# A transformer block in hand-ordered beats: maxima rows sent first, attention rows normalised and transposed earlier

## The chip, the cores and the metric

The kernel runs on one core of one Trainium2 chip. The metric is the device time of one execution in microseconds (us), the median of several runs. The profiles are one execution each.

## The reference

One diffusion-transformer block over a batch of 16 sequences of 256 tokens with 256 channels and 16 heads of 16 channels, all in fp32. Biases, and the first line's `silu`, stand as in the reference:

```python
shift_a, scale_a, gate_a, shift_m, scale_m, gate_m = split(silu(c) @ W_mod + b_mod, 6)
q, k, v = heads(modulate(ln(x), shift_a, scale_a) @ W_qkv + b_qkv)
x = x + gate_a * (softmax(q k^T / 4) v @ W_proj + b_proj)         # self-attention
q = heads(ln(x) @ W_qc + b_qc);  k, v = heads(ln(context) @ W_kvc + b_kvc)
x = x + softmax(q k^T / 4) v @ W_cproj + b_cproj                  # attention to 256 context rows
x = x + gate_m * (gelu(modulate(ln(x), shift_m, scale_m) @ W_mlp1 + b_mlp1) @ W_mlp2 + b_mlp2)
```

## The kernel before

The work is cut into 32 **units**: for every batch row one self-attention (`s`) and one attention to the context (`c`). The order is s0 to s3, then s4, c0, s5, c1 and so on to s15, c11, and then c12 to c15. So from unit 4 on, `s` and `c` alternate up to unit 27 and the rest are `c`. After the units comes the MLP over all batch rows; the set-up before them and a small part of the MLP lie beside the first and last units.

A unit takes eight **beats**; `beat(n, k)` issues everything that belongs to beat k of unit n. Each of TensorE, VectorE (DVE), ScalarE (ACT), GpSimd (POOL) and SyncE (SP) gets its instructions in exactly the order in which the Python code issues them (`InOrder`, lines 39 to 53), and goes through them in that order. So the place of a call in `beat` is its place in the queues of all engines that it uses, and moving a call past another one moves it there too.

Several units are in work at once. In beat k of unit n:

- `visit(n, k)` (lines 1011 to 1026) issues the scores `s` of four heads of unit n+1, for one half of its tokens, and takes their maxima on DVE (`mx`, in `s_tile`); then the transposed scores `st` of two heads of unit n. These contain a row of ones times a row of negative maxima, so that ACT can take the exponential (`pt`) of all of it in one instruction. `st` and `s` have one PSUM buffer each, so scores wait for the maximum of the beat before.
- Beats 0 and 4 hold `av_part`: the products of `pt` and the values (`o`), copied to `oT` by ACT.
- Beats 1 and 5 transpose the maxima (`psm`); `m_send` negates them (`m`) and sends two rows into the queries by DMA from SP. Those sent in beat 1 are read by `st` in beats 4 to 7 of the same unit, those of beat 5 in beats 0 to 3 of the next.
- Beats 6 and 2 transpose the attention result of unit n (first half) and unit n-1 (second half) back to tokens (`psA`); `norm` divides by the sum that came along as a seventeenth column (`rc`, then `A`, on DVE).
- `aT` is the second transposition of unit n-1 (`psT_as`, `psT_ac`), of `A` to channels: `halves()` on TensorE, `evac()` on ACT (`y_as`, `y_ac`), `cut()` on POOL, which splits it into a high and a low part (`xTh`, `xTl`). The projection `ps_P` of beat 7 and of beat 1 of the next unit reads both.
- The layer norm of an `s` or a context input (`ln[0]`), its transposition `T[0]` (`psT_s`, `psT_c`) and the layer norm and transposition of the query rows of a `c` unit (`ln[1]`, `T[1]`: `rs_q`, `xn_q`, `psT_q`) run two to four units ahead. For batch rows 0, 1, 14 and 15 the latter are `late`: `ln[1]` in beat 4, `T[1]` in beat 6 of the same unit (units 2, 4, 27 and 28).
- `Q`, `K`, `V` are the projections for units n+2 and n+3 (`ps_q`, `ps_k`, `ps_v`), in twelve matmuls a half. `high()` and `low()` make their two parts (`h_`, `l_`), `send_high()` and `send_low()` issue four and two DMAs on SP. `load(u)` issues the load of a later unit's input.

Projections and transpositions use 64 of the 128 rows of TensorE each; `lane0` works on one half and `lane1` on the other. `beside(a, b)` interleaves two lists, one for each half, by counted steps: a projection matmul counts 1, a transposition `HALF`.

```python
HALF = 0.53
def beside(a, b):
    ab, at = [chain(*a), chain(*b)], [0, 0]
    while min(at) < 1e9:
        i = at[1] < at[0]
        at[i] += next(ab[i], 1e9)
```

`take(x, 5)` is the next five steps of a list; what is left goes to the next beat (`rest_x`, `rest_y`). The two halves of one transposition write one PSUM bank, and the second half waits for the last instruction of the first (`half_turns`, line 322). PSUM for transpositions, `psm` and `o` comes from two buffers used in turn (`SHORT`), that for projections from two others (`LONG`).

Of the kernel before, what the change touches and what calls it, by code (L numbers as in the profile page):

```python
# [21 lines left out]
def pixart_block(  # L22
# [45 lines left out]
    def ps_gen(name, tag=None):  # L68


        if tag is None and ps_turn[0] is not None:
            ps_turn[0] ^= 1
            tag = (SHORT, LONG)[ps_turn[0]]
        tag = tag or SHORT
        return psum.tile([P, 512], F32, tag=tag, name=name, bufs=2)
# [25 lines left out]
    def tok(ap, b):  # L101
        return ap[b].rearrange("(t p) h -> p t h", p=P)

    def load_x(b):
        X[b] = work.tile([P, NT, H], F32, tag="x", name=f"x_{b}", bufs=5)
        SP.dma_start(X[b], tok(x, b))
# [344 lines left out]
    def take(it, n):  # L451
        for _ in range(n):
            yield next(it, 1)
# [8 lines that stand above are left out]
# [82 lines left out]
    def load(u):  # L544
        if u.kind == "s":
            load_x(u.b)
        else:
            u.ct = work.tile([P, NT, H], F32, tag="c", name=f"c_{u.b}")
            SP.dma_start(u.ct, tok(ctxt, u.b))
# [148 lines left out]
    def m_send(u, hf):  # L698
        m = work.tile([P, P], F32R, tag="m", name=f"m_{u.n}_{hf}", bufs=1)
        at = 96 * hf  # L700
        ACT.mul(m[at:at + 16], u.pm[at:at + 16, :P], -1.0)
        for par in range(2):
            SP.dma_start(u.q[par * 64 + 63:par * 64 + 64, 4 * hf:4 * hf + 4, :].bitcast(F32),
                         m[at + par * 8:at + (par + 1) * 8].bitcast(F32))

    def t_part(u, pair, par, st):


        for c in range(NT):
            PE.matmul(st[:, par, c * N:(c + 1) * N],  # L710
                      u.k[par * 64:par * 64 + 64, pair, c * P:(c + 1) * P],
                      u.q[par * 64:par * 64 + 64, pair, :], start=True, stop=True)
            if c == 0:
                yield
        yield

    def exp(u, pair, st):
        u.pt[pair] = work.tile([P, 2, NT, N], F32, tag="pt", name=f"pt_{u.n}_{pair}", bufs=5)
        ACT.activation(u.pt[pair].rearrange("p r c n -> p (r c n)"), st.rearrange("p r n -> p (r n)"),
                       AF.Exp, scale=SCALE)  # L720
# [9 lines left out]
    def in_turn(*pieces):  # L730

        for _ in range(2):
            for f in pieces:
                next(f)
# [273 lines left out]
    def unit(n):  # L1008
        return units[n] if 0 <= n < nu else None

    def visit(n, k, home=sp):


        v, e = unit(n + 1), k
        s = []
        if v:
            s = [s_tile(v, e // 2, par, e % 2, par, home) for par in range(2)]
        if n < 0:
            in_turn(*s)
            return  # L1020
        bank = sp if n == nu - 1 and k % 2 else st
        t = [t_part(units[n], k, par, bank) for par in range(2)]
        in_turn(*s)
        in_turn(*t)
        later.append(lambda: exp(units[n], k, bank))

    none = (), ()
    rest_x = rest_y = iter(())

    def beat(n, k):  # L1030
        nonlocal rest_x, rest_y
        if n < 0:
            visit(n, k, (st, sp)[k % 2])
            return
        cur, prev, nxt = unit(n), unit(n - 1), unit(n + 1)
        q2, q3, q4 = (v if v and v.n >= m else None
                      for v, m in zip(map(unit, (n + 2, n + 3, n + 4)), (1, 2, 3)))
        p1, p2, p3 = (v and v.post for v in map(unit, (n - 1, n - 2, n - 3)))
        apart = n > nu - 4
        if n - 2 > nu - 5:  # L1040
            p2 = None
        if n - 3 > nu - 5 or p3 and p3.hurry:
            p3 = None
        lc = q4 if q4 and q4.kind == "c" else None
        ls = q4 if q4 and q4.kind == "s" else None
        lx = q3 if q3 and q3.kind == "c" else None
        late = lx and lx.b in (0, 1, B - 2, B - 1)
        early = lc if lc and lc.b not in (0, 1, B - 2, B - 1) else None
        if k == 0 and q2:
            q2.K.high()  # L1050
            q2.K.send_high()
        if k == 2 and p2:
            p2.end()
        if k == 4 and q2:
            q2.Q.high()
            q2.Q.send_high()
        home = sp
        if nxt and n * 8 + k >= nu * 8 - 17 and k % 2:
            home = ps_gen("s0", LONG), ps_gen("s1", LONG)
        visit(n, k, home)  # L1060
        exps()
        if k == 0:
            if prev:
                av_part(prev, 2)
                av_part(prev, 3)
            if q2:
                q2.K.low()
                q2.K.send_low()
            if p3:
                p3.add()  # L1070
            if ls and n > 0:
                load(ls)
            if lc:
                lc.ln[0].steps[0]()
            if p1:
                p1.gate()
        elif k == 1:
            m = m_halves(cur, 1) if cur else none
            x, y = lane0(q2 and q2.Q), lane1(p2)
            beside([m[0], x], [take(y, 4), m[1], y])  # L1080
            if cur:
                m_send(cur, 1)
            if lc:
                lc.ln[0].steps[1]()
                lc.ln[0].steps[2]()
        elif k == 2:
            T = q3.T[0].halves() if q3 else none
            A = p1.halves(1) if prev else none
            x, y = lane0(q2 and q2.V), lane1(q2 and q2.Q)
            beside([T[0], take(x, 5), A[0]], [A[1], take(y, 5), T[1]])  # L1090
            rest_x, rest_y = x, y
            if q3:
                q3.T[0].evac()
                q3.T[0].cut()
            if p2 and p2.hurry:
                p2.add()
        elif k == 3:
            if prev:
                p1.norm(1)
            beside([rest_x], [rest_y])  # L1100
        elif k == 4:
            if cur:
                av_part(cur, 0)
                av_part(cur, 1)
            if q2:
                q2.Q.low()
                q2.Q.send_low()
            if p3:
                p3.store()
            if late:  # L1110
                for f in lx.ln[1].steps:
                    f()
            if ls and not late:
                ls.ln[0].steps[0]()
                ls.ln[0].steps[1](False)
        elif k == 5:
            m = m_halves(nxt, 0) if nxt else none
            aT = p1.aT.halves() if prev else none
            x, y = lane0(q3 and q3.K), lane1(q2 and q2.V)
            beside([m[0], take(x, 4), aT[0], take(x, 3)], [aT[1], take(y, 1), m[1], take(y, 6)])  # L1120
            rest_x, rest_y = x, y
            if prev:
                p1.aT.evac()
                p1.aT.cut()
            if nxt:
                m_send(nxt, 0)
            if ls and late:
                for f in ls.ln[0].steps:
                    f()
            elif ls:  # L1130
                ls.ln[0].pow()
                ls.ln[0].steps[2]()
            if early:
                early.ln[1].steps[0]()
            v = unit(n + 5)
            if v and v.kind == "c":
                load(v)
        elif k == 6:
            if cur:
                cur.post.begin()  # L1140
            T = lx.T[1].halves() if lx else none
            A = cur.post.halves(0) if cur else none
            beside([A[0], take(rest_x, 5), T[0]], [T[1], take(rest_y, 5), A[1]])
            if q2:
                q2.V.keep()
            if early:
                early.ln[1].steps[1]()
                early.ln[1].steps[2]()
            if prev and apart:
                p1.proj(0)  # L1150
                p1.proj(1)
        elif k == 7:
            beside([lane0(None if apart else p1)], [lane1(q3 and q3.K)])
            if lx:
                lx.T[1].evac()
                lx.T[1].cut()
            if prev and apart:
                p1.end()
                p1.add()
                p1.store()  # L1160
            if cur:
                cur.post.norm(0)
# [97 lines left out]
```

## Time and profile before

| | |
|---|---|
| median of 3 runs | 805.89 us (802.38 to 806.07) |
| profiled execution | 800.28 us, span 798.2 us |
| mean granted TensorE clock | 0.995 |
| busy share of the span | TensorE 96%, DVE 74%, ACT 70%, POOL 66% |
| unit 0 begins / MLP alone begins | about 37 us / about 602 us |

A busy share is a mean over parts with different limits; a step of the loop is judged by which engine ends last in its beat. The page's rows give the granted clock in tenths for 40 slices of the span. In a row of a timeline stand the start and the duration in us, engine, line, operation, `out<-in` tiles, shapes and the count of merged instructions; in brackets the engine's idle time before it and what ended that. In a row of windows stand the stretch, its length, the busy time of each engine with its count of instructions, the granted clock, the DMA share and GB/s. In a row of waits stand who waited for whom, the total in us, the times and the longest. All operations are recorded under one line (51, in `InOrder`), so rows are told apart by their tiles.

### The profile page before, as it was taken

The page shows a single profiled execution, that of the slowest core. Times are in us where ns is not written, and L with a number is a line of the kernel's source. Part 1 is how long each engine was busy: PE and PEld are TensorE (multiplying, and loading weights), DVE is VectorE, ACT ScalarE, POOL GpSimd, SP SyncE. Part 2 cuts the span into 40 slices and gives each one's busy share as a digit, 9 for nine tenths or more (in the row PEclk, how much of TensorE's full clock was granted, in tenths as well). Part 3 has the DMA queues.
Part 4 walks back from the last instruction along what each step waited for, and adds up shares of the span by engine and source line. Part 5 has one row for each costly group of instructions (what it writes and reads, how often), then busy time and mean ns, then how long its engine had stood idle before and what let it go on. Part 6 is the DMA issues. An engine that isn't in the chain of part 4 may idle for free.

```text
span 798.2 us, 24978 instructions
## 1 busy us (share of the span) xinstructions
PE 766.0 (96%) x10066; PEld 656.9 (82%) x10066; DVE 589.3 (74%) x1027; ACT 562.0 (70%) x961; POOL 528.4 (66%) x497
## 2 busy tenths in 40 slices
PE   8999899999999999999999999989889999999997
PEld 8778777887877887877888878767669999999997
DVE  5877678888888888888888898776664656656662
ACT  4268587887877877888788888767556666666663
POOL 6756858595766858567595877864546656666653
PEclk9999899999999999999999999999999999999999
DMA  6554344434354544535435554534211321312211
GB/s 208 143 159 123 107 110 121 121 109 144 104 143 108 146 127 109 158 96 146 123 109 150 144 151 136 148 100 115 74 43 42 93 61 60 80 60 61 81 42 52
DMA packets 89942, 87.96 MB, mean 110 GB/s; under 512 B 9506, under 2 KB 85572, under 8 KB 89828
## 3 DMA queue, kind: packets, MB, share of 16 engines
q1 hardware_dynamic: 89364, 85.58, 38.2%
q8 instruction: 80, 1.31, 0.7%
q0 software_dynamic: 192, 0.52, 0.2%
q14 instruction: 34, 0.28, 0.1%
q10 hardware_dynamic: 272, 0.26, 0.1%
HBM read 26.97 MB, written 8.46 MB: 44 GB/s over the span
## 4 chain that ended last, share of the span: by engine, by line
PE 63%; DVE 15%; POOL 9%; issue 5%; ACT 5%; DMA 2%; SPq 1%; POOLq 0%; ACTq 0%; DVEq 0%
PE o L51 14%; PE s L51 12%; PE st L51 7%; DVE mx L51 7%; DVE xn_m L51 4%; PE ps_P_s L51 3%; PE ps_P_c L51 3%; PE ps_v_c L51 3%; POOL hl L51 3%; PE ph L51 3%; PE ps_v_s L51 2%; POOL x L51 2%; PE ps_kc L51 2%; PE ps_q L51 2%; PE ps_qc L51 2%
## 5 line engine op out<-in xcount | busy, mean ns | idle before, releaser
L51 DVE TENSOR_REDUCE mx<-s 128x4 f32<-128x1024 f32 (+1 forms) x257 | 308.3, 1201 | 98.0 <-PE s L51 94.7
L51 ACT ACTIVATE pt<-st 128x1024 f32<-128x1024 f32 x252 | 258.5, 1026 | 49.2 <-PE st L51 37.8
L51 PE MATMUL s<-big 63*128 63x256 f32 (+1 forms) x1024 | 123.8, 314 | 12.0 <-DVE mx L51 10.9
L51 POOL TENSOR_TENSOR hl<-hf,hh 128x512 fp32r<-128x512 f32 x64 | 89.0, 1402 | 54.4 <-ACT hh L51 54.2
L51 PE MATMUL o<-pt,v 128*32 128x256 f32 x2048 | 123.8, 382 | 0.4 <-DVE A_c L51 0.4
L51 PEld LDWEIGHTS s<-big 63*128 63x128 f32 (+1 forms) x1024 | 81.1, 187 | 50.0 <-DVE mx L51 22.3
L51 PE MATMUL st<-big 64*128 64x256 f32 (+1 forms) x1024 | 110.1, 284 | 4.7 <-ACT pt L51 3.1
L51 PEld LDWEIGHTS o<-pt,v 128*32 128x32 f32 x2048 | 60.4, 109 | 41.7 <-PE st L51 0.7
L51 PEld LDWEIGHTS st<-big 64*128 64x128 f32 (+1 forms) x1024 | 83.4, 187 | 8.2 <-ACT pt L51 3.7
L51 ACT ACTIVATE hf<-ph,bT 128x256 f32<-128x256 f32 x120 | 50.3, 473 | 27.6 <-PE ph L51 27.4
L51 ACT COPY oT<-o 128x512 f32<-128x512 f32 x63 | 36.9, 586 | 45.9 <-PE o L51 45.9
L51 ACT ACTIVATE hh<-ph,bT 128x256 fp32r<-128x256 f32 x120 | 50.4, 472 | 22.8 <-PE s L51 8.3
L51 PE MATMUL ph<-wqch,wself 128*128 128x256 f32 x256 | 51.5, 284 | 0.0
L51 PE MATMUL ph<-wkch,wself 128*128 128x256 f32 x256 | 51.4, 285 | 0.0
L51 PE MATMUL s<-big,hh 128*128 128x256 f32 x256 | 46.7, 281 | 0.0
L51 PE MATMUL st<-big,hh 128*128 128x256 f32 x256 | 46.5, 281 | 0.0
L51 DVE TENSOR_SCALAR xn_m<-x,mv_m,rs_m 128x256 f32<-128x256 f32 x32 | 38.4, 1239 | 10.8 <-POOL rs_m L51 10.8
L51 POOL CAST xTh_ac<-y_ac 128x512 fp32r<-128x512 f32 x15 | 9.2, 614 | 54.5 <-ACT y_ac L51 54.5
L51 PE MATMUL ps_k<-xTh_s,wself 64*128 64x256 f32 (+1 forms) x232 | 42.8, 298 | 0.0
L51 POOL CAST xTh_c<-y_c 128x512 fp32r<-128x512 f32 x16 | 9.8, 610 | 48.8 <-ACT y_c L51 48.8
L51 PEld LDWEIGHTS ph<-wqch,wself 128*128 128x128 f32 x256 | 41.6, 189 | 0.4 <-issue 0.4
L51 PEld LDWEIGHTS ph<-wkch,wself 128*128 128x128 f32 x256 | 41.5, 189 | 0.3
(226 smaller groups left out, 2553.0 us busy)
## 6 DMA issues: line engine op xcount, KB each, us to landing
big<-h_kc SPq DMA_DIRECT2D x64, 128.0 KB
big<-h_qc SPq DMA_DIRECT2D x64, 128.0 KB
big<-h_k SPq DMA_DIRECT2D x62, 128.0 KB
big<-h_q SPq DMA_DIRECT2D x62, 128.0 KB
big<-l_k SPq DMA_DIRECT2D x32, 128.0 KB
big<-l_q SPq DMA_DIRECT2D x32, 128.0 KB
c<-in_ctx_dram SPq DMA_DIRECT2D x16, 256.0 KB
g<-gd SPq DMA_DIRECT2D x16, 256.0 KB
```

Source lines behind the costliest of these rows:

```text
L51: i = f(*a, **k)
```

## The change

Four things move; no instruction is added or removed, and the sizes stay.

1. In beat 1, `m_send(cur, 1)` stands ahead of `q2.K.send_low()` and `load(ls)`, which move from beat 0 to after it.
2. `p1.norm(1)` moves from after `visit(n, 3)` to before it: on DVE, `rc` and `A` of the second half stand ahead of the maximum of beat 3.
3. `p1.aT`, its transpositions, its copy and its cut, moves from beat 5 to beat 3.
4. The halves of transpositions in beats 2, 3, 5 and 6 stand at other places of their lists; beat 5 takes eight steps of the projections and leaves four to beat 6, where it took seven and left five.

```diff
@@ beat(n, k), ahead of the visit
+        if k == 3 and prev:
+            p1.norm(1)
         visit(n, k, home)
         exps()
@@ k == 0
             if q2:
                 q2.K.low()
-                q2.K.send_low()
             if p3:
                 p3.add()
-            if ls and n > 0:
-                load(ls)
@@ k == 1
             if cur:
                 m_send(cur, 1)
+            if q2:
+                q2.K.send_low()
+            if ls and n > 0:
+                load(ls)
@@ k == 2
-            beside([T[0], take(x, 5), A[0]], [A[1], take(y, 5), T[1]])
+            beside([T[0], take(x, 1), A[0], take(x, 4)], [take(y, 4), T[1], take(y, 1), A[1]])
@@ k == 3
+            aT = p1.aT.halves() if prev else none
+            beside([take(rest_x, 7), aT[0]], [take(rest_y, 3), aT[1], take(rest_y, 4)])
             if prev:
-                p1.norm(1)
-            beside([rest_x], [rest_y])
+                p1.aT.evac()
+                p1.aT.cut()
@@ k == 5
-            aT = p1.aT.halves() if prev else none
-            beside([m[0], take(x, 4), aT[0], take(x, 3)], [aT[1], take(y, 1), m[1], take(y, 6)])
+            beside([m[0], take(x, 8)], [take(y, 5), m[1], take(y, 3)])
-            if prev:
-                p1.aT.evac()
-                p1.aT.cut()
@@ k == 6
-            beside([A[0], take(rest_x, 5), T[0]], [T[1], take(rest_y, 5), A[1]])
+            beside([T[0], A[0], take(rest_x, 4)], [take(rest_y, 4), T[1], A[1]])
```

## The prediction

> **What bounds the kernel now.** I read the page first, then the waits, then the timeline of one unit, engine by engine. The page gives the shares and the granted clock; the waits name the pair of engines that holds the loop.
>
> ```profile
> PE 766.0 (96%) x10066; PEld 656.9 (82%) x10066; DVE 589.3 (74%) x1027; ACT 562.0 (70%) x961; POOL 528.4 (66%) x497
> PEclk9999899999999999999999999999999999999999
> PEld s L51 <- DVE mx L51: 22.3, 52, 1.7
> ```
>
> TensorE is busy for 96% of the span, so only stretches where it waits, or is held by another engine, can be shortened. The wait that holds it inside the loop is the scores (s) on the maximum (mx). The next rows are unit 13, whose keys and values come from the context; beats 2 to 6 begin just ahead of each mx.
>
> ```profile
> 270.00 1.22 DVE L51 TENSOR_REDUCE mx<-s 128x4 f32<-128x1024 f32 x1
> 271.84 1.23 DVE L51 TENSOR_REDUCE mx<-s 128x4 f32<-128x1024 f32 x1 [0.62 <-PE s L51]
> 272.98 0.25 DVE L51 RECIPROCAL rc_s<-psA_s 128x16 f32<-128x16 f32 x1
> 273.26 0.42 DVE L51 TENSOR_TENSOR A_s<-psA_s,rc_s 128x256 f32<-128x256 f32 x1
> 273.66 1.23 DVE L51 TENSOR_REDUCE mx<-s 128x4 f32<-128x1024 f32 x1
> 276.26 1.22 DVE L51 TENSOR_REDUCE mx<-s 128x4 f32<-128x1024 f32 x1 [0.59 <-PE s L51]
> 278.28 1.23 DVE L51 TENSOR_REDUCE mx<-s 128x4 f32<-128x1024 f32 x1
> ...
> 271.27 0.22 PE L51 MATMUL psA_s<-ident,oT 64*128 64x64 f32 x1
> 271.31 0.49 PE L51 MATMUL s<-big 63*128 63x256 f32 x4
> 273.12 0.50 PE L51 MATMUL s<-big 63*128 63x256 f32 x4 [0.25 <-DVE mx L51]
> ```
>
> From mx to mx the beats take 1.84, 1.82, 2.60 and 2.02 us. Scores of 0.49, a start 0.04 later (271.31 + 0.49 = 271.80, mx at 271.84) and a maximum of 1.23 make a cycle that TensorE cannot undercut: about 1.82. Beats 2 and 3 lie on this floor; in beat 3 TensorE even idles 0.25. Beat 4 is TensorE's own (32 matmuls of o), and beat 5 is 0.20 above the floor. So a step has a price in beat 3 if it delays mx, and a gain in beat 5 if it lightens TensorE.
>
> **Part 1: the second normalisation ahead of the maximum of beat 3.** Now rc and A follow mx of beat 3 and cost nothing: beat 4 is TensorE's. Moved ahead, they wait for the last transposition of psA in beat 2, and behind them wait mx and so the scores of beat 4. From rc to the next mx is 273.66 - 272.98 = 0.68, while DVE's idle time there is 0.62 and partly over before psA is done. The psA transpositions end at 271.27 + 0.22 = 271.49. The re-placed halves of beat 2 change that:
>
> ```profile
> 269.76 0.59 ACT L51 COPY t_c<-ps_P_c 128x512 f32<-128x512 f32 x1 [0.16 <-PE ps_P_c L51]
> 270.40 0.38 PE L51 MATMUL ps_v_c<-wvch,xTh_c 64*128 64x256 f32 x1
> 271.87 0.27 PE L51 MATMUL ps_v_c<-wvcl,xTh_c 64*128 64x256 f32 x1
> ...
> 272.58 0.28 PE L51 MATMUL ps_v_c<-wvch,xTl_c 64*128 64x256 f32 x1
> ```
>
> The first V matmul waits for t_c (269.76 + 0.59 = 270.35). Before, both lists of beat 2 stood still then; after, three Q matmuls are issued ahead of that point. The pace is (272.58 - 271.87) / 6 = 0.12 a matmul, and the code counts a transposition at 0.53 of one, 0.06. From 270.40 on, the second list still holds two matmuls and eight transpositions, 0.74; the last starts at 271.08 and ends at 271.30. I take 271.37, between that and 271.49, because the halves now run beside matmuls and not beside each other. Then mx of beat 3 starts at 271.37 + 0.04 + 0.68 = 272.09, or 0.25 later than now. Bounds: 0.06 if psA is done when mx of beat 2 ends (271.22 + 0.68), 0.37 at 271.49. TensorE's beat 3, with seven matmuls and four transpositions a half (9.1 x 0.12 = 1.1 after 0.5 of scores and exponent matmuls), stays under the new 2.07. It reaches the transposes of A after three matmuls, at 271.87 + 0.36 = 272.23, when A is ready (272.08), so the V and Q matmuls queued behind them do not wait. The cost is paid in 25 units (1, 3, 5 to 26, 29): 25 x 0.25 = **+6.2 us** (1.5 to 9.2).
>
> **Part 2: the attention rows leave beat 5.**
>
> ```profile
> 275.85 0.59 ACT L51 COPY oT<-o 128x512 f32<-128x512 f32 x1 [0.80 <-PE o L51]
> 276.49 0.27 PE L51 MATMUL psT_as<-ident,A_s 64*128 64x64 f32 x1
> 277.72 0.27 PE L51 MATMUL ps_v_c<-wvch,xTh_c 64*128 64x256 f32 x1
> 273.12:281.56 8.44, 8.36 (x129) 6.86 (x130) 7.64 (x14) 6.81 (x11) 7.16 (x8) 1.00 0.36 96
> sum 110.39, PE 109.32 PEld 89.69 DVE 97.12 ACT 88.76 POOL 91.67; mean PE 8.41 PEld 6.90 DVE 7.47 ACT 6.83 POOL 7.05
> ```
>
> psT_as needs the PSUM buffer that the copy oT frees at 276.44, so TensorE starts it late and ends its list at 277.72 + 0.27. In beat 3 it takes the buffer of the transposes psT_s instead, copied by then. Without it beat 5 falls to the floor: 2.02 to 1.82. Another 0.04 goes in beat 4, because y_s, now transposed sooner, lets the exponential of beat 3 end sooner. So beats 4 to 7 of such a unit take 8.20 and not 8.44. The sum row is the 13 odd units 1 to 25: 110.39 - 13 x 8.20 = **-3.8 us**. On ScalarE the copy of the attention rows (0.59) now stands ahead of Q's high part and the exponential of beat 4; the idle 0.80 ahead of oT covers it. If that cover were gone, beat 5 would take 0.59 more.
>
> The other units, which prepare a self-attention unit, are the windows of beats 4 to 7 of units 14 and 10, with the sum of the 11 even units 6 to 26:
>
> ```profile
> 289.92:298.56 8.64, 8.64 (x136) 7.09 (x138) 7.33 (x15) 6.82 (x12) 4.35 (x5) 1.00 0.48 134
> 221.44:230.79 9.35, 8.98 (x136) 7.30 (x138) 7.56 (x15) 7.05 (x12) 4.33 (x5) 1.00 0.47 131
> sum 97.41, PE 96.88 PEld 79.48 DVE 81.31 ACT 76.88 POOL 47.73; mean PE 8.81 PEld 7.23 DVE 7.39 ACT 6.99 POOL 4.34
> 217.81 1.20 SPq L51 DMA_DIRECT2D big<-l_k  x2
> 219.73 1.42 SPq L51 DMA_DIRECT2D big<-m  x2
> 222.31 0.35 PE L51 MATMUL st<-big 64*128 64x256 f32 x1 [0.37 <-ACT h_q L51]
> ```
>
> **Part 3: maxima rows first on SP.** In unit 10 the m rows are issued at 219.73, after key parts and the load, and beat 4's st, which reads them, starts only at 222.31, half a microsecond late. (The releaser named had long ended; I read it as m's landing.) Sent ahead of the two low key parts and the load, they go at about 217.81, 1.9 sooner, and the stall ends. What is late next is DVE's mx of beat 5, behind the statistics of x: unit 14, which has no stall, still takes 8.64. So nine units come to 8.64 and the two without statistics (24, 26) to 8.20: 9 x 8.64 + 2 x 8.20 = 94.2, **-3.2 us**. The key parts moved back are read a unit later, and x, loaded about one beat later, is read in beat 4: nothing is paid there, as long as x lands within three microseconds.
>
> **Part 4: POOL.** The cut of the attention rows moves ahead of rs_q and xn_q in the four units (2, 4, 27, 28) that normalise the query rows in beat 4; there TensorE already waits for xn_q.
>
> ```profile
> 84.24 0.71 POOL L51 TENSOR_TENSOR rs_q<-rs_q,mhalf 128x2 f32<-128x2 f32 x1 [1.28 <-DVE rs_q L51]
> 513.88 0.71 POOL L51 TENSOR_TENSOR rs_q<-rs_q,mhalf 128x2 f32<-128x2 f32 x1 [0.73 <-DVE rs_q L51]
> 517.07 0.61 POOL L51 CAST xTh_as<-y_as 128x512 fp32r<-128x512 f32 x1
> 517.77 1.30 POOL L51 TENSOR_TENSOR xTl_as<-y_as,xTh_as 128x512 fp32r<-128x512 f32 x1
> 535.06 0.71 POOL L51 TENSOR_TENSOR rs_q<-rs_q,mhalf 128x2 f32<-128x2 f32 x1
> ```
>
> The cut takes 2.0 (517.07 to 519.07); the idle time ahead of rs_q takes in 1.28 of it in unit 2, 0.73 in unit 27 and none in unit 28; unit 4, where it is longer than the cut, loses nothing. Delay 0.7 + 0 + 1.3 + 2.0 = 4.0, less about 0.5 for lighter beats 6: **+3.5 us** (0 to 4).
>
> **Part 5: the last two units.**
>
> ```profile
> 574.12 0.46 PE L51 MATMUL psT_ac<-ident,A_c 64*128 64x64 f32 x4
> 575.83 0.94 PE L51 MATMUL ps_warm<-wz 128*128 128x128 f32 x6 [0.73 <-ACT y_ac L51]
> 589.22 0.39 PE L51 MATMUL ph<-wkch,wself 128*128 128x256 f32 x1
> 589.98 0.42 DVE L51 TENSOR_TENSOR A_c<-psA_c,rc_c 128x256 f32<-128x256 f32 x1
> ```
>
> In unit 30 the transposes leave a beat in which ps_warm waits 0.73 for their copy, about -1.0. In unit 31 they move ahead of ph, which could start at 589.22, and wait for A_c (590.40): +1.2. Together **+0.2**.
>
> **Sum.** 6.2 - 3.8 - 3.2 + 3.5 + 0.2 = +2.9 us on the profiled execution's 800.28 (its span 798.2 and 2.1 around it): 803.2. The runs shown have a median of 805.89, 0.7% above that execution, so I forecast 805.89 + 2.9 = 808.8. About 4 us, 0.5%, is what a measurement of this kernel can tell from no change: the forecast is no change.
>
> **The rivals.** *Slower: the halves run badly beside matmuls.* In beat 5 the mixed list took 276.49 to 277.99, 1.50, for 9.1 counted steps, 0.16 a step and not 0.12. If beat 2 goes at that rate, the 6.2 steps after 270.40 take 1.0, psA ends near 271.6, and mx of beat 3 is 0.5 late: 25 x 0.25 more, 815. It decides wherever psA ends after 271.49. Against it: the wait for oT's buffer explains part of the slow list.
>
> *The clock.* After the stalls of unit 2 the granted clock fell; after equal stalls of unit 28 it did not:
>
> ```profile
> 86.00:90.00 4.00, 2.94 (x33) 2.63 (x32) 1.46 (x4) 1.61 (x2) 3.92 (x5) 0.55 0.40 132
> 90.00:94.00 4.00, 4.00 (x47) 3.78 (x48) 2.26 (x4) 2.22 (x4) 3.81 (x5) 0.60 0.02 4
> 533.00:537.00 4.00, 2.48 (x37) 1.98 (x33) 3.08 (x9) 1.91 (x5) 3.79 (x4) 1.00 0.59 160
> ```
>
> Part 4 lengthens unit 28's stall by 2.0. A fall as in unit 2 loses up to 0.45 x 4 + 0.40 x 4 = 3.4; part of that lies in the stall itself, and I take 2: 810.8. [...]
>
> *Faster: the normalisation fits DVE's gap.* If psA is done by 271.22, Part 1 costs 1.5 and not 6.2; if POOL, relieved of its wait for y_ac, also has the cut out of the way in the late units, Part 4 goes to 0: 808.8 - 4.7 - 3.5 = 800.6. For it: the 0.62 of idle DVE. Against: t_c holds V until 270.40.
>
> *The m rows change nothing,* since st waits for something else: Part 3 is lost, 812.
>
> **How the numbers follow.** Forecast 0.42 (of it 0.33 same, 0.06 slower, 0.03 faster); bad mixing 0.18, slower; clock 0.10 (0.06 slower, 0.04 same); fits the gap 0.20 (0.14 faster, 0.06 same); m rows 0.10 (0.07 slower, 0.03 same). Faster 0.17, same 0.46, slower 0.37. The range runs from the faster case, 800, to a little past bad mixing, 816. The forecast's own range, from its bounds, is 804 to 812.
>
> **What would show it.** Right: in ordinary units rc and A stand between the maxima of beats 2 and 3, beat 3 takes about 2.07 and beat 5 of odd units 1.82; st in beat 4 never starts more than 0.4 after its scores; rs_q of units 27 and 28 waits behind xTl_as and xTl_ac. Wrong: beat 3 still at 1.84, or beat 2 grown above 1.9; beat 5 still at 2.0; unit 10 still above 9 us in beats 4 to 7; a second stretch of low clock.

## The result and the profile after

The changed kernel takes 811.34 us (median of 8 runs, 808.78 to 815.38) against 803.12 us before (8 runs, 800.61 to 806.07): a ratio of 1.0105, interval 1.0076 to 1.0135. The time lies in the range, but the forecast called no change is wrong: the kernel is slower by 8 us, about 1%. The two profiled executions, 811.77 and 800.28 us, stand 11.5 us apart, and in what follows this difference is taken apart. Two rows of the page of the kernel after, then three of its waits (who waited for whom, us in all, times, longest):

```profile
PE 773.1 (95%) x10066; PEld 662.9 (82%) x10066; DVE 588.7 (73%) x1027; ACT 561.4 (69%) x961; POOL 529.2 (65%) x497
PEclk9999899999999999999999999998999999999999
```

```profile
PEld s L51 <- DVE mx L51: 33.5, 86, 2.2
DVE rc_c L51 <- PE psA_c L51: 7.9, 14, 1.3
DVE rc_s L51 <- PE psA_s L51: 5.8, 15, 0.4
```

The work is the same; what grew is a wait. The weight loads of scores wait for maxima for 33.5 us where it was 22.3, and `rc` now waits for the transposed attention result, 29 times. The clock row has a second slice of 8. Unit 13 shows the new order, first on DVE, then on TensorE:

```profile
272.28 1.23 DVE L51 TENSOR_REDUCE mx<-s 128x4 f32<-128x1024 f32 x1
273.93 0.26 DVE L51 RECIPROCAL rc_s<-psA_s 128x16 f32<-128x16 f32 x1 [0.43 <-PE psA_s L51]
274.22 0.42 DVE L51 TENSOR_TENSOR A_s<-psA_s,rc_s 128x256 f32<-128x256 f32 x1
274.56 1.22 DVE L51 TENSOR_REDUCE mx<-s 128x4 f32<-128x1024 f32 x1
276.38 1.22 DVE L51 TENSOR_REDUCE mx<-s 128x4 f32<-128x1024 f32 x1 [0.60 <-PE s L51]
```

```profile
272.70 0.38 PE L51 MATMUL ps_v_c<-wvch,xTh_c 64*128 64x256 f32 x1
272.92 0.21 PE L51 MATMUL psA_s<-ident,oT 64*128 64x64 f32 x1
273.10 0.22 PE L51 MATMUL psA_s<-ident,oT 64*128 64x64 f32 x1
273.14 0.36 PE L51 MATMUL ps_qc<-xTh_q,wqch 64*128 64x256 f32 x1
273.38 0.27 PE L51 MATMUL psA_s<-ident,oT 64*128 64x64 f32 x1
273.62 0.22 PE L51 MATMUL psA_s<-ident,oT 64*128 64x64 f32 x1
```

The maximum of beat 2 ends at 273.51; `psA` is done at 273.62 + 0.22 = 273.84, `rc` starts 0.43 late, and the maximum of beat 3 comes 2.28 after that of beat 2, where it was 1.84. The next rows are sums of windows; a beat begins with the first weight load of its scores. Of the kernel before: beats 2 and 3 of the 25 ordinary units, and beats 0 and 1 of the 13 odd and 11 even units. Of the kernel after: beats 2 and 3 of the 25, beats 4 to 7 of the odd and then of the even units, and beats 0 and 1 of both.

```profile
sum 93.29, PE 86.53 PEld 78.26 DVE 68.98 ACT 79.40 POOL 60.55; mean PE 3.46 PEld 3.13 DVE 2.76 ACT 3.18 POOL 2.42
sum 110.03, PE 110.03 PEld 84.58 DVE 97.80 ACT 85.94 POOL 94.14; mean PE 4.58 PEld 3.52 DVE 4.08 ACT 3.58 POOL 3.92
```

```profile
sum 103.94, PE 102.20 PEld 92.17 DVE 82.80 ACT 84.62 POOL 72.79; mean PE 4.09 PEld 3.69 DVE 3.31 ACT 3.38 POOL 2.91
sum 106.46, PE 102.94 PEld 83.59 DVE 86.59 ACT 85.03 POOL 78.44; mean PE 7.92 PEld 6.43 DVE 6.66 ACT 6.54 POOL 6.03
sum 95.54, PE 89.66 PEld 73.33 DVE 74.25 ACT 73.23 POOL 56.78; mean PE 8.15 PEld 6.67 DVE 6.75 ACT 6.66 POOL 5.16
sum 111.42, PE 110.92 PEld 84.83 DVE 97.47 ACT 87.24 POOL 85.94; mean PE 4.62 PEld 3.53 DVE 4.06 ACT 3.63 POOL 3.58
```

So beats 2 and 3 cost 10.65 (103.94 - 93.29), the odd units gain 3.93 (110.39 before), the even ones 1.87 (97.41 before), and beats 0 and 1 cost 1.4. The four late units, cut in the same way, cost 1.7 in beats 2 and 3, 3.6 in beats 4 to 7 and 0.7 in beats 0 and 1; unit 30 gains 1.45, unit 31 loses 1.36. Unit 29's later beats and the set-up take the last -0.7.

Two losses have no forerunner in the prediction's sum. In unit 24, SP hands over the maxima later, and `st` in beat 0 of unit 25 waits for them; in units 12 and 22, the statistics of x wait for its load. SP's issues before, then after, then two of the waits:

```profile
465.06 1.42 SPq L51 DMA_DIRECT2D big<-m  x2
```

```profile
471.18 2.48 SPq L51 DMA_DIRECT2D big<-m  x2
474.84 0.61 PE L51 MATMUL st<-big 64*128 64x256 f32 x4 [0.44 <-DMA big<-m]
433.60 0.75 DVE L51 BATCH_NORM_STATS2 st_s<-x 128x6 f32<-128x256 f32 x2 [0.49 <-DMA x<-in_x_dram]
```

Beat 6 of unit 24 begins at 464.06 before and at 470.01 after: the first of the two issues starts 1.17 into it instead of 1.00, and both take 2.48 instead of 1.42 (the first alone 1.74 instead of 0.69). Beat 0 of units 5, 9, 18, 24, 25 and 27 takes 2.7 to 3.4 instead of 2.6. The clock, in windows:

```profile
88.20:91.70 3.50, 3.50 (x43) 3.50 (x41) 1.59 (x3) 1.73 (x3) 2.75 (x3) 0.51 0.40 132
125.80:129.20 3.40, 3.40 (x38) 3.40 (x34) 1.81 (x3) 1.69 (x3) 2.73 (x3) 0.50 0.42 139
525.20:528.60 3.40, 3.23 (x36) 3.23 (x38) 0.79 (x1) 0.89 (x2) 0.12 (x1) 0.50 0.29 78
545.70:552.50 6.80, 5.11 (x48) 4.53 (x50) 2.42 (x3) 1.99 (x3) 4.59 (x5) 0.50 0.21 71
```

Before, there was one such stretch in the loop (86.4 to 93.2); now there are four, in units 2, 4, 27 and 28, 17 us of half clock in place of 6.8.

### The profile page after: what moved, and what is told of

Read it like the earlier page. It is cut to its first block, busy times and chain, and to the rows that moved or that the text cites. A ratio compares the mean times of both kernels' runs of the same rounds, so it can differ in the third digit from the quotient of the medians.

```text
span 809.7 us, 25080 instructions
## 1 busy us (share of the span) xinstructions
PE 773.1 (95%) x10066; PEld 662.9 (82%) x10066; DVE 588.7 (73%) x1027; ACT 561.4 (69%) x961; POOL 529.2 (65%) x497
## 4 chain that ended last, share of the span: by engine, by line
PE 52%; DVE 22%; POOL 10%; issue 6%; ACT 5%; DMA 3%; SPq 1%; POOLq 0%; ACTq 0%
PE o L51 11%; PE s L51 11%; DVE mx L51 10%; PE st L51 6%; DVE xn_m L51 4%; PE ps_P_s L51 3%; POOL hl L51 3%; PE ph L51 2%; PE ps_qc L51 2%; POOL x L51 2%; PE ps_P_c L51 2%; PE ps_q L51 2%; PE ps_v_c L51 2%; DVE xTf_m L51 2%; PE ps_kc L51 1%
## 5 line engine op out<-in xcount | busy, mean ns | idle before, releaser
L51 PE MATMUL s<-big 63*128 63x256 f32 (+1 forms) x1024 | 126.2, 319 | 16.9 <-DVE mx L51 14.5
L51 PEld LDWEIGHTS s<-big 63*128 63x128 f32 (+1 forms) x1024 | 80.5, 188 | 61.7 <-DVE mx L51 33.5
L51 PE MATMUL st<-big 64*128 64x256 f32 (+1 forms) x1024 | 108.0, 284 | 3.4 <-ACT pt L51 2.1
L51 PE MATMUL ps_q<-xTh_s,wself 64*128 64x256 f32 (+1 forms) x240 | 43.4, 293 | 0.4 <-DVE l_q L51 0.4
L51 POOL TENSOR_SCALAR xn_q<-x,mv_q,rs_q 128x256 f32<-128x256 f32 x32 | 39.0, 1226 | 1.7
```

Of the source, the lines that this page charges most:

```text
L51: i = f(*a, **k)
```

## The experiments

My theory for the first four is that most of the loss sits in the new wait of the maximum of beat 3 for `psA`, and goes if `psA` ends sooner. Its rivals put it on the other moved steps: on SP's order, or on TensorE's lists as such. Two edits undo or isolate a part, two change the list; the later ones take away what then is left. Ratios are to the kernel before on the same chip, whose median was 801.12 for e1 to e4, 800.44 for e5 to e8 and 801.31 for e9 to e12.

**e1: only the normalisation, on the kernel before.**

```diff
+        if k == 3 and prev:
+            p1.norm(1)
         visit(n, k, home)
...
-            if prev:
-                p1.norm(1)
             beside([rest_x], [rest_y])
```

> The kernel before with one edit: the second normalisation stands ahead of the maximum of beat 3, and nothing else moves. Theory A (the price sits here): beats 2 and 3 of the 25 ordinary units grow by 0.35 to 0.45 us each, as in the changed kernel, because rc waits for the transposes psA and the maximum waits behind it; the time rises by 9 to 11 us (1.1 to 1.4%). Rival B (the price comes from the transposes that now lie beside matmuls and in beat 3): the old list of beat 2 has psA done in time, beats 2 and 3 grow by under 0.1, and the time stays within 2.5 us of the kernel before.

806.84 us, ratio 1.0069 (1.0049 to 1.0089): 5.7 us. DVE of unit 13, then the sum of beats 2 and 3 of the 25 units:

```profile
269.92 1.23 DVE L51 TENSOR_REDUCE mx<-s 128x4 f32<-128x1024 f32 x1
271.48 0.26 DVE L51 RECIPROCAL rc_s<-psA_s 128x16 f32<-128x16 f32 x1 [0.34 <-PE psT_s L51]
272.11 1.21 DVE L51 TENSOR_REDUCE mx<-s 128x4 f32<-128x1024 f32 x1
```

```profile
sum 101.15, PE 86.55 PEld 78.30 DVE 82.43 ACT 86.66 POOL 66.96; mean PE 3.46 PEld 3.13 DVE 3.30 ACT 3.47 POOL 2.68
```

The row names `psT_s`, which runs beside `psA` on the other half and ends with it (at 271.45 and 271.44). With the list of before, the maximum of beat 3 is 0.35 late (2.19 after that of beat 2), and the 25 units pay 7.9 in these two beats, 0.31 a unit. They get part of it back in beat 4, 2.9 us over the loop, where stalls of `st` shrink; I read it as the m rows having more time to land. So the step alone is a loss, smaller than expected in all, but larger per unit than the prediction's 0.25.

**e2: only SP's order, on the kernel before.**

```diff
 # k == 0
-                q2.K.send_low()
...
-            if ls and n > 0:
-                load(ls)
...
 # k == 1
                 m_send(cur, 1)
+            if q2:
+                q2.K.send_low()
+            if ls and n > 0:
+                load(ls)
```

> The kernel before with one edit: on SP the maxima rows of beat 1 go ahead of the low key parts and the load of x. Theory A: the stall of st in beat 4 of the even units goes, but the load comes too late in some units for the statistics in beat 4 and DVE waits for it there: beats 4 to 7 of the 11 even units lose 1.5 to 2.5 us in all and a beat 5 of about 3 us appears in one or two of them; time 1 to 3 us under the kernel before. Rival B (st waited for something else than the m rows): beat 4 stays at 2.8 to 3.3 in units 8, 10, 12, 18 and 20 and the time does not move.

799.36 us, ratio 0.9979 (0.9964 to 0.9995), a small gain. Beats 4 to 7 of the even units, 97.41 before:

```profile
sum 94.99, PE 94.96 PEld 78.21 DVE 80.39 ACT 75.16 POOL 48.10; mean PE 8.63 PEld 7.11 DVE 7.31 ACT 6.83 POOL 4.37
```

The stalls of `st` in beat 4 are gone and 2.4 us are gained: theory A holds for Part 3, and SP's order isn't where the loss comes from. All 11 units take 8.61 to 8.65, as unit 14 did before. The long beat 5 that I expected didn't come: here no statistics of x wait for their load.

**e3: the change with the old list of beat 2.**

```diff
-            beside([T[0], take(x, 1), A[0], take(x, 4)], [take(y, 4), T[1], take(y, 1), A[1]])
+            beside([T[0], take(x, 5), A[0]], [A[1], take(y, 5), T[1]])
```

> The changed kernel with the list of beat 2 as it was before, so that transposes lie beside transposes. Theory A (the halves re-placed in beat 2 are not what costs; both lists end with the transposes psA): beats 2 and 3 together stay at 4.10 to 4.20 us in ordinary units, and the time is within 3 us of the changed kernel, some 8 us over the kernel before. Rival B (transposes beside matmuls run slowly and this alone makes psA late): beats 2 and 3 fall to about 3.95, and the time to about 4 us under the changed kernel.

808.86 us, ratio 1.0094 (1.0070 to 1.0117). Beats 2 and 3 of the 25 units:

```profile
sum 101.41, PE 99.41 PEld 90.08 DVE 81.58 ACT 82.43 POOL 67.51; mean PE 3.98 PEld 3.60 DVE 3.26 ACT 3.30 POOL 2.70
```

8.1 over the kernel before, 0.32 a unit, much as in e1, where the whole change has 10.65. The new list of beat 2 is worth only 2.5 us of the loss in these beats; the other 8.1 come with `psA` at the end of either list. By the ratios the whole kernels lie only 0.9 us apart, within their intervals.

**e4: the change with `A` first in beat 2's lists.**

```diff
-            beside([T[0], take(x, 1), A[0], take(x, 4)], [take(y, 4), T[1], take(y, 1), A[1]])
+            beside([A[0], T[0], take(x, 5)], [take(y, 3), A[1], take(y, 2), T[1]])
```

> The changed kernel with another list in beat 2: the transposes psA first, then psT, the V matmuls last on their half, so that psA is done about 1 us after the beat began and V does not wait for t. Theory A (the maximum of beat 3 is late because psA ends last): rc and A then follow the maximum of beat 2 at once, the maximum of beat 3 starts at most 0.15 us later than in the kernel before, beats 2 and 3 take 3.75 to 3.9 us, and the time is 6 to 9 us under the changed kernel, level with the kernel before. Rival B (a normalisation of 0.68 us in that gap costs its own length wherever psA ends): beats 2 and 3 stay above 4.05 and the time within 3 us of the changed kernel.

803.91 us, ratio 1.0032 (1.0016 to 1.0047). TensorE's last `psA` of unit 13, DVE behind it, and the sum of beats 2 and 3:

```profile
269.94 0.28 PE L51 MATMUL psA_s<-ident,oT 64*128 64x64 f32 x2
```

```profile
269.25 1.23 DVE L51 TENSOR_REDUCE mx<-s 128x4 f32<-128x1024 f32 x1
270.39 0.25 DVE L51 RECIPROCAL rc_s<-psA_s 128x16 f32<-128x16 f32 x1
271.09 1.23 DVE L51 TENSOR_REDUCE mx<-s 128x4 f32<-128x1024 f32 x1
```

```profile
sum 92.73, PE 92.45 PEld 87.73 DVE 82.31 ACT 79.56 POOL 60.36; mean PE 3.70 PEld 3.51 DVE 3.29 ACT 3.18 POOL 2.41
```

`psA` ends 0.26 before the maximum does, `rc` follows it at once, the maximum of beat 3 keeps its 1.84, and the 10.65 us are gone, to 0.6 below before. This settles Part 1: not the normalisation's place costs, but where `psA` ends under it. By the ratios the kernel is 5.9 us faster than the whole change, just short of the 6 to 9 expected, and still 2.6 us over the kernel before, not level with it. What is left of the loss lies elsewhere: the late units, beats 0, the waits for x in beat 5 of even units, and unit 31, which here loses 4.3 and not 1.4. TensorE there:

```profile
591.63 1.40 PE L51 MATMUL psT_ac<-ident,A_c 64*128 64x64 f32 x8 [1.17 <-DVE A_c L51]
592.96 0.58 PE L51 MATMUL ph<-wkch,wself 128*128 128x256 f32 x1
```

**e5: e4 with the load ahead of the low key parts.**

```diff
                 m_send(cur, 1)
+            if ls and n > 0:
+                load(ls)
             if q2:
                 q2.K.send_low()
-            if ls and n > 0:
-                load(ls)
```

> The kernel with psA first in beat 2 (all of the change but its list of beat 2), and the load of x now goes on SP right behind the maxima rows, ahead of the two low key parts. Theory A (DVE waits in beat 5 of some even units for x, which the change loads 1.2 us later than need be): beat 5 of units 10, 12, 14 and 22 falls from 2.5 to 3.4 back to 2.28, and the time by 1.5 to 2.5 us, to 0.999 to 1.002 of the kernel before. Rival B (x comes late because its transfer is slow, wherever it is issued): these beats stay and the time stays at 1.003 of the kernel before.

800.98 us, ratio 1.0012 (0.9999 to 1.0025), by the ratios 1.6 us below e4. Beat 5 of units 10 and 12 falls to 2.28, but 14 and 22 keep 2.76 and 3.35. So the load's place is part of the cause. In unit 22 SP issues the load at 420.24 in 0.43, and the statistics wait for it until 425.79: there theory B holds, the transfer itself is late. Why it is late stays open.

**e6: e4 with the late units' cut back in beat 5, behind the query norm, and unit 31's transposes there too.**

```diff
-            aT = p1.aT.halves() if prev else none
+            aT = p1.aT.halves() if prev and nxt else none
...
-            if prev:
+            if prev and nxt:
                 p1.aT.evac()
-                p1.aT.cut()
+                if not late:
+                    p1.aT.cut()
 # k == 5
+            if prev and not nxt:
+                for _ in chain(*p1.aT.halves()):
+                    pass
+                p1.aT.evac()
+            if prev and (late or not nxt):
+                p1.aT.cut()
```

> The kernel with psA first in beat 2, and in units 2, 4, 27 and 28 the cut of the attention rows stands in beat 5 again, behind rs_q and xn_q on POOL; in unit 31 the transposes of A stand in beat 5 again. Theory A (the cut ahead of rs_q delays xn_q, which TensorE waits for): units 2, 27 and 28 lose 4 us in all and unit 31 1.2 or more; the time falls by 4 to 6 us, to 0.996 to 0.999 of the kernel before. Rival B (these units are longer because the granted clock falls, whatever POOL does): the stalls shrink but two or more stretches of low clock stay at 500 to 600 us, and the time falls by under 2 us.

798.24 us, ratio 0.9975 (0.9960 to 0.9991): below the kernel before and by the ratios 4.6 us below e4. Unit 31 is as long as in the kernel before (4.3 less than e4), and the late units lose 1.8 of their 5.3. They don't come back to before, though POOL's chain does: `xn_q` of unit 28 starts 3.5 us into beat 5, as before (4.75 after the whole change). Three stretches of half clock remain (0.50 from 84.9 to 91.7, 515.0 to 518.4 and 535.5 to 542.3), two of them beyond 500 us: theory A's gain came, and theory B's sign with it.

**e7: e4 with the m rows of beat 5 ahead of the low query parts and the store.**

```diff
 # k == 4
-                q2.Q.send_low()
-            if p3:
-                p3.store()
 # k == 5
                 m_send(nxt, 0)
+            if q2:
+                q2.Q.send_low()
+            if p3:
+                p3.store()
```

> The kernel with psA first in beat 2, and in beat 5 the maxima rows go on SP ahead of the two low query parts and the store of x. Theory A (st in beat 0 waits for the maxima rows sent in beat 5 of the unit before, which SP reaches later since the copy of the attention rows stands ahead of Q's high part): beat 0 of units 3, 6, 9, 19, 24 to 27 falls from 2.7 to 3.5 back to 2.55 to 2.65, and the time by 3 to 4 us, to 0.998 to 1.000 of the kernel before. Rival B (beat 0 is held by an exponential or by the keys of the next unit): beat 0 stays and so does the time, at 1.003.

826.16 us, ratio 1.0325 (1.0291 to 1.0359), by the ratios 23 us slower than e4. SP and TensorE around the start of unit 9 (199.68):

```profile
195.61 1.42 SPq L51 DMA_DIRECT2D big<-m  x2
197.14 1.31 SPq L51 DMA_DIRECT2D big<-l_q  x2
200.25 0.50 PE L51 MATMUL s<-big 63*128 63x256 f32 x3 [0.18 <-DMA big<-l_q]
```

Theory A fails; my reading of the slack was wrong. The low query parts of unit n+2 are read by `s` in beat 0 of unit n+1, at the same time as the m rows by `st`; sent last, they hold the scores in nearly every unit: beat 0 grows to 3.1. (Beat 7 grows to 2.35 as well; why was not followed.) SP's queue has no room for this in beats 4 to 7; the low query parts are as urgent as the m rows.

**e8: e5, e6 and e7 together.** Of the three diffs, the lines that matter:

```diff
                 m_send(cur, 1)
+            if ls and n > 0:
+                load(ls)
...
+            if prev and (late or not nxt):
+                p1.aT.cut()
             if nxt:
                 m_send(nxt, 0)
+            if q2:
+                q2.Q.send_low()
+            if p3:
+                p3.store()
```

> The three edits together on the kernel with psA first in beat 2. Theory A (the change is sound, and what it lost was the place of psA in beat 2 and three waits that it made, all independent): the gains add to 8 to 11 us under the kernel with psA first alone, 0.988 to 0.993 of the kernel before and 5 to 8 us under the kernel with the maxima rows first alone. Rival B (removing one wait uncovers another, or the DMA queue only moves the wait): less than 5 us under the kernel with psA first, 0.997 or more of the kernel before.

818.13 us, ratio 1.0242 (1.0210 to 1.0273). Theory B by the time, but e7's edit carries it; the gains of the others show in their places (unit 31 and the late units as in e6, beats 5 of units 12, 14 and 22 all at 2.28).

**e9: e6 with e5's load order.** On e6:

```diff
                 m_send(cur, 1)
+            if ls and n > 0:
+                load(ls)
             if q2:
                 q2.K.send_low()
-            if ls and n > 0:
-                load(ls)
```

> The kernel of e6 (rows of A first in beat 2's lists, late units' cut behind the query norm, unit 31's transposes left in beat 5) with the load of the next input right behind the m rows of beat 1, ahead of the low key parts. Theory A: what e6 still loses in beat 5 of even units is the statistics of x waiting for its load: units 12, 14 and 22 took 3.34, 2.75 and 3.00 against 2.28 of the others, 2.3 us in all, and the load one or two issues sooner takes off the half of it or more: 1 to 2 us below e6's 2.9 under the kernel before, so about 797, 4 us under it. Theory B: the load lands late for another reason (the traffic of the transfer itself): the three beats keep their length and the kernel stays where e6 was, 2 to 3 us under the kernel before.

796.40 us, ratio 0.9938 (0.9918 to 0.9959). Beats 5 shorten as expected, but unit 22 keeps 2.99, and long beats 0 remain. The rows that led to e10 are ACT and SP in beats 4 and 5 of unit 8 (from 184.53) and TensorE in beat 0 of unit 9 (from 193.18):

```profile
184.73 0.59 ACT L51 COPY y_ac<-psT_ac 128x512 f32<-128x512 f32 x1
185.21 0.84 ACT L51 ACTIVATE h_q<-ps_q,bqkv 128x256 fp32r<-128x256 f32 x2
185.71 3.78 SPq L51 DMA_DIRECT2D big<-h_q  x4
194.13 0.50 PE L51 MATMUL st<-big 64*128 64x256 f32 x3 [0.23 <-DMA big<-m]
```

The copy stands ahead of `h_q`, so SP's first issue comes 1.18 into beat 4; the four issues take 3.78 (the last alone 1.89), and the m rows behind them come too late.

**e10: e9 with the copy behind Q's high part.**

```diff
             q2.Q.high()
             q2.Q.send_high()
+        if k == 4 and prev and nxt:
+            p1.aT.evac()
+            if not late:
+                p1.aT.cut()
...
 # k == 3
-            if prev and nxt:
-                p1.aT.evac()
-                if not late:
-                    p1.aT.cut()
```

> e9 with the copy of the attention rows (y) and its cut behind Q's high part in beat 4 and not ahead of it in beat 3. Theory A: beats 0 that still run to 2.7 to 3.5 (units 5, 8, 9, 11, 21, 26) wait for the m rows of beat 5, which SP issues late because the copy y (0.59, from 0.20) stands ahead of h_q on ScalarE (0.68 and not 0.12 to 0.30) and so ahead of the high query parts' sends: with the sends 0.5 sooner these stalls, 2.7 us over the kernel before, mostly end, and the kernel comes out 2 us under e9. Theory B: SP is late from the count and the length of its issues (0.55 to 0.6 each, some 1.1 to 1.7), the copy's place changes nothing: within 0.7 us of e9, beat 0 as in e9.

793.12 us, ratio 0.9897 (0.9879 to 0.9915), 3.3 us below e9. The same rows (beat 4 from 183.27), and the sum of beats 0 and 1 of the 24 units, 112.76 in e9 and 110.03 in the kernel before:

```profile
183.41 0.84 ACT L51 ACTIVATE h_q<-ps_q,bqkv 128x256 fp32r<-128x256 f32 x2
184.13 0.59 ACT L51 COPY y_ac<-psT_ac 128x512 f32<-128x512 f32 x1
183.91 2.49 SPq L51 DMA_DIRECT2D big<-h_q  x4
```

```profile
sum 110.51, PE 110.02 PEld 84.40 DVE 97.85 ACT 87.47 POOL 86.27; mean PE 4.58 PEld 3.52 DVE 4.08 ACT 3.64 POOL 3.59
```

SP starts 0.64 into the beat, half a microsecond sooner, and nearly all long beats 0 end (units 24 and 27 keep theirs): theory A. ScalarE's copy, which I had covered with idle time ahead of `oT`, delayed SP and through it the m rows. In unit 8 this is only part of it, since the fourth issue takes 0.60 here and 1.89 in e9. That the copy counts is shown by the whole kernel: the six runs (792.01 to 794.00) all lie below those of e9 (795.37 to 797.64).

**e11: e9 with only the store behind the m rows of beat 5.**

```diff
 # k == 4
-            if p3:
-                p3.store()
 # k == 5
                 m_send(nxt, 0)
+            if p3:
+                p3.store()
```

> e9 with the store of the finished rows (p3.store, one issue of 0.55) behind the m rows of beat 5 and not ahead of them; the low query parts stay where they are. Theory A (SP's queue sets when the m rows go): one issue less ahead of them in the units that store, so the beats 0 behind even units shorten: 1 to 2 us under e9. Theory B: the m rows wait for the maxima's copy m (ready at 2.0 in beat 5) and not for the queue: within 0.7 us of e9.

794.03 us, ratio 0.9912 (0.9889 to 0.9936). Beats 0 and 1 sum to 110.69: theory A here too, though less surely, since the interval overlaps that of e9. One issue fewer on SP seems to do what half a microsecond of head start does, and unlike the low query parts the store has no reader in the next beats.

**e12: e10 and e11 together.**

> Both edits of e10 and e11 on e9: the candidate for the fastest. If both A's hold, all long beats 0 go and the kernel is 2 to 4 us under e9, near 794; if only SP's queue counts, as e11; if neither, as e9. A rival for all three: units whose beats 0 are long differ from run to run with single long issues (1.1 to 1.7), and then the four kernels differ by less than their intervals.

791.01 us (five runs, 790.43 to 791.41), ratio 0.9872 (0.9853 to 0.9891). It beats both kernels: 10 us below the one before, and 5.4 below e9, where I expected 2 to 4. The rival (chance between runs) falls, as its interval lies apart from that of e9. Beats 0 and 1 of the 24 units:

```profile
sum 109.53, PE 109.53 PEld 84.10 DVE 97.66 ACT 87.31 POOL 85.26; mean PE 4.56 PEld 3.50 DVE 4.07 ACT 3.64 POOL 3.55
```

No idle TensorE is left in beats 0 and 1 (109.53 busy of 109.53). So the change, with its steps' order mended, gains some 10 us; as it stood, the waits that its own moves set up hid that. Not all of the 10 need be the change's own: the new places of the store (e11) and of `psA` in beat 2 (e4) were not tried on the kernel before.

## Why the prediction was right or wrong

**Part 1, the step that failed.** Its sign and mechanism are as forecast; its size was 10.65 and not 6.2, and outside its own bounds of 1.5 to 9.2. The term at fault is the end of `psA`, which the re-placed halves were to bring forward. Measured from the end of the maximum of beat 2, it was put at 0.15 later (271.37 against 271.22) and came 0.33 later (273.84 against 273.51). The delay is the forecast 0.25 plus these 0.18: 0.43, times 25. The old list costs less than the new one: 0.32 a unit in e3. The rest of the working held: `psA` to next maximum took 0.72 (0.04 + 0.68 forecast). Of the list behind the first V matmul I forecast 0.68 from its start to the last transposition's start, and it took 0.92 (272.70 to 273.62). I had counted steps at a pace of 0.12. The rows suggest a wait for about half of the 0.24: the second half of `psA` may start only after the last instruction of the first (273.10 + 0.22 = 273.32), and starts at 273.38, 0.24 behind the matmul ahead of it (273.14), while in the old list one half had gone early. Another 0.10 is the first step, 0.22 long (272.70 to 272.92). No run isolates that wait, but e3 and e4 show that the place of `psA` in the list sets the price. The rival of bad mixing put it at 12.5 us in all, nearer than the forecast, and by its own condition it is the one that came: `psA` ends 0.33 after the maximum, and 271.49 would be 0.27. For its reason, transpositions beside matmuls, e3 leaves at most 2.5 of the 10.65. That the late units pay the same delay (+1.7) was left out.

**Part 2** was right: -3.9 for -3.8, beat 5 on its floor at 1.82. But its copy did not cost nothing: it moved SP half a microsecond back (e10), which shows only in beats 0 and only where SP had no slack. I had named a cover for ScalarE and not followed the queue behind `h_q`.

**Part 3** was right in its step and too large by 1.3: in e2 it gave 2.4, after the change 1.87 of 3.2. What failed is "nothing is paid there, as long as x lands within three microseconds": in units 12 and 22 it doesn't (SP starts the issue at 256.59 and 429.45, and the statistics wait for it until 260.98 and 433.60), and DVE's statistics stand ahead of the maximum. SP's order alone does not do that, since in e2 no statistics wait.

**Part 4** came out at 3.6 for 3.5, but not for its reason alone. Units 27 and 28 lost 1.4 and 2.0, forecast at 1.3 and 2.0, unit 2 gained 0.9, and unit 4, forecast at nothing, lost 1.0, with its clock at 0.50 from 125.8 to 129.2. In e6, POOL's delay was taken away and unit 28 still took 1.7 more than before (13.68 against 12.01 in beats 4 to 7), at half clock from 535.5 to 542.3. So the size was partly luck: the clock rival, priced at 2 and held apart, happened inside this term.

**Part 5** was right: -1.45 for -1.0, and +1.36 for +1.2.

**The sum.** Against +2.9 the profiles differ by 11.5: 4.5 from Part 1's size, 1.7 from Part 1 in the late units, 2.1 from beats 0 and 1, 1.3 from Part 3, and -1.0 from the rest. The medians differ by 8.2, because the execution profiled before was a short one of its kernel. "A second stretch of low clock" and "beat 2 grown above 1.9" (1.96 in even units) were the named signs of a wrong forecast, and both came; the second was a poor sign, since even units had 1.91 to 1.93 before.

## What to carry to other kernels

When a step is moved ahead of a critical one, find the exact instruction whose end it waits for, and move that one forward too: here the same normalisation cost 10.65 us with its input at the end of a list and nothing with it at the start. When a step moves on one engine, follow the instruction that it displaces down to the queues: in e9 a copy of 0.59 us, with idle time behind it, stood ahead of `h_q`, and SP's first issue came 1.18 into the beat; with the copy behind `h_q` (e10) it came at 0.64, the m rows that `st` reads four beats after the copy were no longer late in most units, and the kernel was 3.3 us faster. In a DMA queue order by the reader's beat, not by the name: two parts that are read in the same beat cost 23 us here when one was put behind the other (e7).

## What the runs showed of the hardware

In the two profiled executions the granted clock of the loop was 1.00, and 0.50 in these stretches: before, one from 86.39 to 93.21; after the change four, from 88.28, 125.83, 525.19 and 545.67, which lasted 3.41, 3.41, 3.41 and 6.83 us.

A stall of one length had two outcomes. Unit 31 has the same rows after the change and in e4, with the same stall of 1.17 us, which ends at 600.61 and at 591.63. The 3.4 us up to its end and the 3.4 behind it, after the change and then in e4:

```profile
597.20:600.60 3.40, 2.18 (x20) 1.29 (x18) 2.50 (x10) 2.05 (x2) 1.76 (x2) 1.00 0.08 18
600.60:604.00 3.40, 3.33 (x32) 2.71 (x36) 1.50 (x4) 0.85 (x2) 1.70 (x3) 1.00 0.27 76
```

```profile
588.20:591.60 3.40, 2.21 (x20) 1.32 (x18) 2.52 (x10) 2.05 (x2) 1.76 (x2) 1.00 0.11 25
591.60:595.00 3.40, 3.31 (x17) 3.01 (x18) 0.73 (x2) 0.59 (x1) 1.29 (x3) 0.52 0.20 69
```

TensorE is busy for 2.18 and 2.21 us ahead of the stall's end. After the change the clock stayed at 1.00, the eight `psT_ac` behind the stall took 0.98, and the unit lost 1.36. In e4 the clock was at 0.50 from 591.7 on and still at 595.4, the same eight took 1.40, and the unit lost 4.3. Nor does TensorE's busy time alone tell the two apart in the kernel before: 1.92 busy in the 3.41 us from 82.97 were followed by 0.50, and 1.93 in the 3.41 us from 533.53 by 1.00. What decides was not shown.

SP's issues are uneven: the same four high query parts took 3.78 us of issue in e9 and 2.49 in e10, the two m rows 2.48 after and 1.42 before; each time one single issue makes nearly all of the difference (1.89 against 0.60, and 1.74 against 0.69). In both places `st` then waited for the m rows: for 0.23 us in e9, four beats after the high query parts, and for 0.44 in the changed kernel, two beats after the m rows' issue. What makes an issue long was not tried.
